# A decoder layer whose kernel plans its own order: loads of inputs get an earliest start, and the stage ranks change

## The chip, the cores and the metric

The kernel runs on one core of a Trainium2 chip. The metric is the device time of one execution in microseconds. Three runs of the kernel before gave 891.12, 892.58 and 895.39 us; the median is 892.58. One more execution was recorded by the hardware profiler, and all views below come from that one.

The core has these engines, each with its own program in order: TensorE (PE; its weight loads are shown apart as PEld), VectorE (DVE), ScalarE (ACT), GpSimd (POOL) and SyncE (SP). SP here only issues transfers. Sixteen DMA engines carry out the transfers that SP and POOL issue.

## The reference

Sixteen sequences of 256 tokens by 256 channels go through one layer, all in float32. There are three sub-layers, each added to its input and then normalised:

```python
x = layernorm(x + attn(x, ...))            # causal depthwise conv, cos/sin features, cumulative sums, gate
x = layernorm(x + xattn(x, ctx, ctx, ...)) # autocorrelation by FFT, top 5 shifts, softmax, rolled values
x = layernorm(x + ffn(x, ...))             # 8 experts: (x V) * cumsum(x W), router softmax, projection by U
```

In `ffn`, two branches are computed, of which the second works on inputs that went through one more matrix, `W_inv`:

```python
Q = x @ W_Q.T; K = x @ W_K.T; invQ = Q @ W_inv.T; invK = K @ W_inv.T
out = fused_branch(Q, K, V_fwd, W_fwd, U_fwd, ...) + alpha_bi * fused_branch(invQ, invK, W_inv_exp, V_inv, U_inv, ...)
return out @ W_O.T
```

The kernel multiplies the weight matrices of this chain together first, which it calls folding, so that each branch needs one product per side and expert.

## The kernel before

**The work.** The sequences are handled in eight pairs. For each pair there are seven stages: `front` (input projection, convolution, score weights), `body` (features, cumulative sums, output projection, first layernorm), `context` (spectra of the context's keys and values), `back`, `attention` (the second sub-layer), `router` and `experts` (the third). `fold_weights` runs once. Contexts depend on no other stage; for pairs 1 to 7 (`AHEAD`, line 50) the spectra are stored to scratch tensors in HBM (`kf_away`, `vf_away`) and `back` loads them again before attention.

**The order.** The code of the stages does not run in the order in which it is written. The objects V, S, G, T and Y (for DVE, ACT, POOL, PE and SP) only take notes: each call becomes an operation (`Op`) with a duration, a latency, its predecessors, and a rank from `PLACES` (line 39), which for every stage holds a length and one begin for each pair. `Work.run` (line 385) then plans and issues. It makes three passes (`PASSES`). In each, `forward` (line 264) is a list scheduler: each engine takes the operation of the lowest rank among those that can run, where an operation needs its predecessors done and places free for its tiles. `backward` (line 375) then finds for each operation the latest time at which it could run, walking the operations from the last end to the first and keeping the order on each engine; these times are the ranks of the next pass. The first pass has the ranks of `PLACES`. The pass with the shortest planned span is issued. Each engine's program is then fixed; on the chip, only semaphores for data and buffers hold it up.

**Tiles.** Many tiles share one tag of 18 places, "slab": the raw weights of folding, context tiles (`ct`, `bothc`, `specc`, `ks`), and expert tiles (`e`, `wb`, `h`, `fwT`). Line 407 limits how many of each kind may hold a place. `x` has 7 buffers (`load_x`, line 456), and `xT` has one (line 550).

**The loads of inputs.** On SP's queue are `xT` (one for each pair, 512 KB), `ct` (one for each sequence, 256 KB, line 845) and `in_proj_w`. On POOL's queue are `x` (one for each sequence, 256 KB), the constants and weights of lines 462 to 468 and 716 to 745, and the raw weights of folding (lines 772 and 776). SP also issues the spreads that copy rows of one tile over many partitions of another: `sn` and `ge` (from `zc` and `g`), `ph`, `vh` and `wb`. POOL also issues the stores and reloads of the spectra and the stores of the output.

In the profile nearly every operation has line 399, since the planner issues them all there; tiles tell them apart. `bothc` is made by POOL from `ct`; `w_ps` are the products of folding, which ACT copies out to `w_v`, `w_c`, `w_h` and `u_o`; `sc_ps` and `in_ps` are front's products with `xT`.

Of the kernel before, what the change touches and what calls it, by code (L numbers as in the profile page):

```python
# [36 lines left out]


PLACES = {
    "front": (0.8, 0.85, 4.2, 3.65, 3.95, 4.75, 6.55, 6.1, 7.7),  # L40
    "body": (0, 0.25, 1.4, 3.7, 2.25, 4.35, 5.1, 6.55, 7.1),
    "ctx": (0.55, 0.83, -0.15, 0.45, 0.55, 0.8, 1.0, 1.25, 1.25),
    "back": (0.35, -1.45, -1.5, -2.45, -2.05, 0.65, 1.35, 2.8, 3.6),
    "att": (0.5, 0.6, 0.75, 1.4, 0.05, 4.0, 4.45, 5.55, 6.85),
    "router": (1.75, 1.4, 0.1, 3.0, 3.15, 4.1, 5.5, 7.8, 6.9),
    "expert": (1.03, 3.85, 4.55, 5.7, 5.95, 7.65, 8.25, 8.8, 10.25),
    "fold": (2.4, 0.61),
}
EARLY, SLABS, XT_BUFS, ZC_BUFS, KBUFS, VBUFS, X_BUFS = 3, 18, 1, 6, 2, 3, 7
AHEAD = range(1, NP)  # L50
# [28 lines left out]
class Op:  # L79


    def __init__(self, k, eng, rank):
        self.k, self.eng, self.rank = k, eng, rank
        self.parts, self.mm, self.pre, self.then, self.tiles = [], [], {}, [], []
        self.table, self.shape, self.lock, self.size, self.dur, self.lat = None, None, False, 0, 0.0, 0.0


class Clock:
# [24 lines left out]
class Work:  # L113
# [3 lines left out]


    SETS = {AF.Exp: 0, AF.Sin: 1, AF.Silu: 1, AF.Gelu: 2, AF.Sqrt: 3}
    LEAD = {"PE": 0, "DVE": 85, "ACT": 103, "POOL": 40, "SP": 0}  # L120
    LATE = {"PE": 33, "DVE": 35, "ACT": 35, "POOL": 80, "SP": 40}

# [61 lines left out]
    def note(self, eng, op, issue, args, kw):  # L184
        aps = [v for v in list(args) + list(kw.values()) if isinstance(v, bass.AP)]
        out = kw.get("out", aps[0])
        ins = [v for v in aps if v is not out]
        o = self.last
        if not (eng == "PE" and o and o.eng == "PE" and (self.joins or o.tiles[-1] == out.tensor.name)):
            o = Op(len(self.ops), eng, self.rank)  # L190
            self.ops.append(o)
        self.last = o
        o.parts.append((issue, args, kw))
        d, lat, o.lock = self.cost(eng, op, out, ins)
        if eng == "PE":
            r, c = ins[0].ap[0][1], self.columns(ins[0])
            r0, c0 = ins[0].offset // math.prod(ins[0].tensor.shape[1:]), out.offset // math.prod(out.tensor.shape[1:])
            cells = [(i, j) for i in range(r0 // 32, (r0 + r + 31) // 32) for j in range(c0 // 32, (c0 + c + 31) // 32)]
            o.mm.append((d, cells))
            o.shape = r, c  # L200
        else:
            o.dur, o.lat = d, lat
        if op == "dma_start":
            o.size = 4 * self.columns(out) * out.ap[0][1]
        if op == "activation":
            o.table = self.SETS.get(args[2])
        for ap in ins + [out]:
            t = ap.tensor
            if not hasattr(t, "tag"):
                continue  # L210
            write = ap is out
            p0, p1, f0, f1 = self.box(ap)
            self.tiles.setdefault(t.name, (t, []))[1].append(o)
            keep = []
            for a in self.users.get(t.name, ()):
                q, w, a0, a1, b0, b1 = a
                meets = q is not o and a0 < p1 and p0 < a1 and b0 < f1 and f0 < b1
                if meets and (w or write):
                    o.pre[q] = o.pre.get(q, False) or w
                if not (write and meets and p0 <= a0 and a1 <= p1 and f0 <= b0 and b1 <= f1):  # L220
                    keep.append(a)
            keep.append((o, write, p0, p1, f0, f1))
            self.users[t.name] = keep

            if t.name in o.tiles:
                o.tiles.remove(t.name)
            o.tiles.append(t.name)
# [33 lines left out]
            return 35 if raw and o.eng != "PE" else -q.lat  # L261
        return self.LATE[o.eng]

    def forward(self, rank):
        need = {o: len(o.pre) for o in self.ops}
        ready = dict.fromkeys(self.ops, 0.0)
        can = {e: sorted((rank[o], o.k, o) for o in self.ops if o.eng == e and not o.pre) for e in self.LEAD}
        free = dict.fromkeys(self.LEAD, 0.0)
        held = {"DVE": 0.0, "POOL": 0.0}
        empty = {tag: [0.0] * n for tag, n in self.slots.items()}  # L270
# [3 lines left out]
        last, taken = {}, {}  # L274
# [3 lines left out]
        def wanted(o):  # L278

            names = [name for name in o.tiles if name not in taken]  # L280
            for name in list(names):
                names += [n for n in self.after[name] if n not in taken and n not in names]
            return names

        def room(o):

            r, names = ready[o], wanted(o)
            for name in names:
                tag, kind = self.tiles[name][0].tag, self.kind[name]
                places = empty[tag]  # L290
                n = 1 if len(names) == 1 else sum(self.tiles[q][0].tag == tag for q in names)
                if len(places) < n:
                    return None
                if kind and (name not in turn[kind][-n:] or share[kind] < 1):
                    return None
                if not kind and not self.takes(name, starts):
                    return None
                r = max(r, (places[0] if len(places) == 1 else sorted(places)[n - 1]) + 40)
            return max([r] + [taken[name] for name in o.tiles if name in taken])

        landed = {"SP": 0.0, "POOL": 0.0}
        starts, order = {}, []
        while len(order) < len(self.ops):
            pick = None
            for e, ops in can.items():
                if pick is not None and free[e] >= pick[0]:
                    continue

                t, best, later = free[e], None, []
                for key, k, o in ops:  # L310
                    if best is not None and key > best[0]:
                        break
                    r = room(o)
                    if r is None:
                        continue
                    key += self.swap if o.table is not None and o.table != table else 0.0
                    if r > t:
                        later.append((r, key, k, o))
                    elif best is None or (key, k) < best[:2]:
                        best = key, k, o  # L320
                if best is None:
                    if not later:
                        continue
                    t = min(later, key=lambda c: c[0])[0]
                    best = min(c[1:] for c in later if c[0] <= t)
                if pick is None or t < pick[0]:
                    pick = t, best[2]
            if pick is None:
                raise RuntimeError("nothing can go on")
            t, o = pick  # L330
            e = o.eng
            can[e].remove((rank[o], o.k, o))
            for name in wanted(o):
                tag, kind = self.tiles[name][0].tag, self.kind[name]
                slot = min(empty[tag])
                empty[tag].remove(slot)
                taken[name] = slot + 40
                if kind:
                    turn[kind].remove(name)
                    share[kind] -= 1  # L340
            if o.table is not None and o.table != table:
                t, table = t + 1283, o.table
            if e == "PE" and o.shape != shape:
                t, shape = t + 93, o.shape
# [11 lines left out]
            for name in o.tiles:  # L356
                left[name] -= 1
                last[name] = max(last.get(name, 0.0), end)
                if not left[name]:
                    empty[self.tiles[name][0].tag].append(last[name])  # L360
                    if self.kind[name]:
                        share[self.kind[name]] += 1
            for q in o.then:
                ready[q] = max(ready[q], end + self.gap(o, q, q.pre[o]))
                need[q] -= 1
                if not need[q]:
                    insort(can[q.eng], (rank[q], q.k, q))
        return order, starts, max(end for t, end in starts.values())

    def takes(self, name, starts):  # L370
# [13 lines left out]

    def run(self, passes):
        self.prepare()
        rank, best = {o: o.rank for o in self.ops}, None
        for n in range(passes):
            order, starts, span = self.forward(rank)
            if best is None or span < best[0]:  # L390
                best = span, order, starts
            rank = self.backward(starts, span)
        self.span = best[0]
        self.give(best[1], best[2])

# [863 lines left out]
```

## Time and profile before

| what | value |
|---|---|
| median of three runs | 892.58 us (891.12 to 895.39) |
| the profiled execution | 892.24 us, of which the span is 890.5 us |
| granted TensorE clock, mean of the span | 0.98 |
| matmuls, other instructions of DVE, ACT, POOL | 4500; 1230, 861, 269 |
| DMA traffic | 99.46 MB, mean 112 GB/s |
| traffic by slice, first four slices of 22 us | 294, 346, 101, 56 GB/s |
| of the engines' time, whole span | SP's queue 35.0%, POOL's queue 10.8% |
| of the engines' time, first 45 us | SP's queue 33.9%, POOL's queue 62.5% |
| shares of the chain that ended last | PE 48%, DVE 19%, ACT 15%, DMA 9%, issue 6%, SP's queue 2% |

The page gives for each engine the time in which it was busy, and then cuts the span into 40 slices: each digit is the busy share of a slice in tenths. The row PEclk is the clock that TensorE was granted, in tenths of full speed. The chain of waits is followed back from the last instruction to whatever released each step; its rows give a start, a duration and the step. A row of the list of waits names the engine that waited and its tile, then whom it waited for, the total in microseconds, how often, and the longest.

### The profile page before, as it was taken

How to read it: one execution, taken by the hardware profiler on the slowest of the kernel's cores; microseconds unless marked ns; L12 is line 12 of the kernel's file. 1: busy time of each engine (PE TensorE's matmuls, PEld its weight loads, DVE VectorE, ACT ScalarE, POOL GpSimd, SP SyncE). 2: the span in 40 equal slices, each digit the busy share in tenths (PEclk: the TensorE clock that was granted, in tenths of full speed). 3: DMA queues.
4: the chain of work that ended last, by engine and by line, in shares of the span. 5: the costliest groups of instructions: out<-in, count | busy, mean ns of one | idle time of the engine just before them, and what ended most of it. 6: DMA issues, size and time to landing. Idle time of an engine off the chain costs nothing.

```text
span 890.5 us, 12540 instructions
## 1 busy us (share of the span) xinstructions
PE 830.9 (93%) x4500; PEld 492.8 (55%) x4500; DVE 712.3 (80%) x1230; ACT 581.8 (65%) x861; POOL 239.3 (27%) x269
## 2 busy tenths in 40 slices
PE   4689998999989999998999989997999999999994
PEld 2345554554537655674557535573566557666554
DVE  6489698878999999799898999997999976364241
ACT  3668966896966785689857887677596942322401
POOL 8640485621320123121212311030323111120000
PEclk9899999999999999999999989999999999999998
DMA  9942758443656246514652637236463160050050
GB/s 294 346 101 56 211 130 237 135 140 81 142 120 134 56 97 141 142 36 107 142 119 72 166 67 145 49 63 127 124 138 79 41 149 18 1 118 1 24 96 24
DMA packets 52382, 99.46 MB, mean 112 GB/s; under 512 B 6592, under 2 KB 18928, under 8 KB 52320
## 3 DMA queue, kind: packets, MB, share of 16 engines
q1 hardware_dynamic: 42640, 67.65, 35.0%
q0 software_dynamic: 9680, 31.01, 10.8%
q8 instruction: 35, 0.57, 0.3%
q14 instruction: 27, 0.22, 0.1%
HBM read 28.38 MB, written 11.53 MB: 45 GB/s over the span
## 4 chain that ended last, share of the span: by engine, by line
PE 48%; DVE 19%; ACT 15%; DMA 9%; issue 6%; SPq 2%; POOL 0%; POOLq 0%; DVEq 0%; ACTq 0%
PE u_ps L399 10%; PE v_ps L399 9%; PE c_ps L399 7%; PE h_ps L399 4%; DVE cs L399 4%; ACT cs L399 4%; DVE sn L399 3%; DMA sn<-zc 3%; ACT L399 3%; DVE zc L399 3%; ACT sn L399 3%; PE wo_ps L399 2%; PE roll_ps L399 2%; DMA xT<-in_xT 2%; SPq L399 2%
## 5 line engine op out<-in xcount | busy, mean ns | idle before, releaser
L399 ACT ACT_TABLE_LOAD x89 | 114.2, 1283 | 46.2 <-DVE flmv L399 33.9
L399 PE MATMUL v_ps<-fxT,w_v 128*128 128x512 f32 x256 | 122.9, 614 | 2.5 <-ACT wf L399 2.5
L399 PE MATMUL c_ps<-fcT,w_c 128*128 128x512 f32 x256 | 119.3, 600 | 0.0
L399 PE MATMUL u_ps<-u_o,e 128*128 128x256 f32 x512 | 116.2, 380 | 0.5 <-ACT h L399 0.5
L399 PEld LDWEIGHTS u_ps<-u_o,e 128*128 128x128 f32 x512 | 96.3, 190 | 15.8 <-issue 1.5
L399 DVE SCALAR_TENSOR_TENSOR zc<-in_ps,pv,zc 128x255 f32<-128x255 f32 (+4 forms) x144 | 76.5, 558 | 3.3 <-ACT zc L399 2.7
L399 PEld LDWEIGHTS v_ps<-fxT,w_v 128*128 128x128 f32 x256 | 48.2, 195 | 55.7 <-issue 49.6
L399 PEld LDWEIGHTS c_ps<-fcT,w_c 128*128 128x128 f32 x256 | 47.8, 192 | 54.1 <-issue 50.2
L399 DVE TENSOR_TENSOR_SCAN cs<-again,cs 128x1024 f32<-128x1024 bf16 x32 | 77.3, 2415 | 0.1
L399 DVE TENSOR_TENSOR_SCAN sn<-again,sn 128x1024 f32<-128x1024 bf16 x32 | 76.7, 2396 | 0.1
L399 POOL TENSOR_TENSOR x<-x,bo 128x512 f32<-128x512 f32 x16 | 30.3, 1896 | 140.7 <-DVE bothx L399 125.1
L399 PE MATMUL in_ps<-xT,in_proj_w 128*32 128x256 f32 (+1 forms) x576 | 62.0, 407 | 3.0 <-DVE zc L399 2.0
L399 PE MATMUL kv_ps<-Wkv,specc 128*128 128x512 f32 x128 | 59.2, 601 | 3.9 <-ACT specc L399 3.8
L399 POOL TENSOR_TENSOR pp<-qf,kf 128x256 f32<-128x256 f32 (+1 forms) x32 | 45.0, 1425 | 57.5 <-ACT qf L399 55.4
L399 PE MATMUL h_ps<-fxT,w_h 128*128 128x512 f32 x128 | 59.7, 603 | 0.7 <-ACT specx L399 0.7
L399 ACT ACTIVATE sn<-sn,theta_col 128x512 f32<-128x512 f32 x64 | 44.4, 714 | 21.1 <-DMA sn<-zc 21.1
L399 DVE TENSOR_TENSOR e<-e,v_ps 128x512 f32<-128x512 f32 x64 | 42.7, 673 | 17.0 <-PE v_ps L399 16.9
L399 DVE TENSOR_TENSOR sn<-sn,ge 128x1024 f32<-128x1024 f32 x32 | 41.3, 1292 | 10.3 <-ACT sn L399 7.4
L399 DVE SCALAR_TENSOR_TENSOR cs<-cs,sn 128x1024 f32<-128x1024 f32 x32 | 40.7, 1272 | 10.1 <-ACT cs L399 10.0
L399 POOL TENSOR_TENSOR t<-vf,wf 128x256 f32<-128x256 f32 x32 | 24.6, 788 | 89.5 <-ACT wf L399 64.6
L399 ACT ACTIVATE ge<-sn 128x1024 f32<-128x1024 f32 x32 | 33.8, 1055 | 22.4 <-DVE cs L399 13.8
L399 POOL TENSOR_TENSOR g<-g,zc 128x512 f32<-128x512 f32 x16 | 22.1, 1380 | 96.8 <-ACT g L399 92.9
(217 smaller groups left out, 1633.4 us busy)
## 6 DMA issues: line engine op xcount, KB each, us to landing
sn<-zc SPq DMA_DIRECT2D x64, 256.0 KB
ge<-g SPq DMA_DIRECT2D x64, 256.0 KB
wb<-fwT SPq DMA_DIRECT2D x64, 256.0 KB
ct<-in_ctx SPq DMA_DIRECT2D x16, 256.0 KB
xT<-in_xT SPq DMA_DIRECT2D x8, 512.0 KB
x<-in_x POOLq DMA_DIRECT2D x16, 256.0 KB, 5.0
ph<-sc SPq DMA_DIRECT2D x64, 64.0 KB
vh<-sv SPq DMA_DIRECT2D x32, 128.0 KB
```

What stands on the lines that cost most here:

```text
L399: call(*args, **kw)
```

## The change

Three things change. First, the planner marks as a fetch every transfer whose source is no tile, that is, an input in HBM. In the second and third pass a fetch can't begin before its latest time from the pass before, less 40 us. Second, all eight rows of `PLACES` have new numbers (the length of "fold" is used nowhere, its begin is). Third, `forward` keeps what it found for an engine or an operation until something that was looked at has changed.

```diff
 PLACES = {
-    "front": (0.8, 0.85, 4.2, 3.65, 3.95, 4.75, 6.55, 6.1, 7.7),
-    "body": (0, 0.25, 1.4, 3.7, 2.25, 4.35, 5.1, 6.55, 7.1),
-    "ctx": (0.55, 0.83, -0.15, 0.45, 0.55, 0.8, 1.0, 1.25, 1.25),
-    "back": (0.35, -1.45, -1.5, -2.45, -2.05, 0.65, 1.35, 2.8, 3.6),
-    "att": (0.5, 0.6, 0.75, 1.4, 0.05, 4.0, 4.45, 5.55, 6.85),
-    "router": (1.75, 1.4, 0.1, 3.0, 3.15, 4.1, 5.5, 7.8, 6.9),
-    "expert": (1.03, 3.85, 4.55, 5.7, 5.95, 7.65, 8.25, 8.8, 10.25),
-    "fold": (2.4, 0.61),
+    "front": (0.8, 0.8, 4.55, 3.6, 3.95, 4.75, 6.6, 6.1, 7.7),
+    "body": (0.05, -0.05, 1.4, 3.7, 2.25, 4.4, 5.45, 7.05, 7.25),
+    "ctx": (0.75, 1.48, 0.15, 1.2, 1.3, 1.55, 1.8, 1.9, 2.05),
+    "back": (1.75, -2.35, -2.3, -4.2, -4.15, -1.0, -0.45, 1.1, 2.25),
+    "att": (0.25, 0.6, 0.85, 1.35, 0.3, 3.95, 4.45, 5.7, 7.0),
+    "router": (1.6, 1.35, -0.85, 3.0, 2.5, 3.65, 5.5, 7.7, 6.95),
+    "expert": (1.03, 3.85, 4.5, 5.6, 5.95, 7.45, 8.1, 8.95, 10.25),
+    "fold": (1.0, 0.66),
 }
...
+    AHEAD = 40000.0
...
         if op == "dma_start":
             o.size = 4 * self.columns(out) * out.ap[0][1]
+            o.fetch = not any(hasattr(i.tensor, "tag") for i in ins)
...
-    def forward(self, rank):
+    def forward(self, rank, late=None):
         need = {o: len(o.pre) for o in self.ops}
-        ready = dict.fromkeys(self.ops, 0.0)
+
+        ready = {o: max(0.0, late[o] - self.AHEAD) if late and o.fetch else 0.0 for o in self.ops}
...
+        found, looked, seen, stuck, settled = {}, {}, set(), {}, {}
+        version = dict.fromkeys(empty, 0)
...
-        rank, best = {o: o.rank for o in self.ops}, None
+        rank, late, best = {o: o.rank for o in self.ops}, None, None
         for n in range(passes):
-            order, starts, span = self.forward(rank)
+            order, starts, span = self.forward(rank, late)
             if best is None or span < best[0]:
                 best = span, order, starts
-            rank = self.backward(starts, span)
+            rank = late = self.backward(starts, span)
```

In the lines left out of `forward`, `found` holds an engine's next choice, `stuck` an operation's lack of a place together with the `version` of that tag, and `settled` the earliest start of an operation that needs no new place. They are dropped when a place of the tag is taken or freed, or when a predecessor ends.

More of the change, by code (lines that the diff above doesn't have):

```diff
@@ L85, in __init__ @@
         self.table, self.shape, self.lock, self.size, self.dur, self.lat = None, None, False, 0, 0.0, 0.0
+        self.fetch = False
 class Clock:
@@ L289, in room @@
                 tag, kind = self.tiles[name][0].tag, self.kind[name]
+                seen.add(tag)
                 places = empty[tag]
+                stuck[o] = tag, version[tag]
                 n = 1 if len(names) == 1 else sum(self.tiles[q][0].tag == tag for q in names)
@@ L296, in room @@
                 if not kind and not self.takes(name, starts):
+                    seen.add(None)
+                    stuck[o] = None
                     return None
                 r = max(r, (places[0] if len(places) == 1 else sorted(places)[n - 1]) + 40)
-            return max([r] + [taken[name] for name in o.tiles if name in taken])
+            r = max([r] + [taken[name] for name in o.tiles if name in taken])
+            stuck[o] = None
+            if not names:
+                settled[o] = r
+            return r
         landed = {"SP": 0.0, "POOL": 0.0}
+        found, looked, seen, stuck, settled = {}, {}, set(), {}, {}
+        version = dict.fromkeys(empty, 0)
         starts, order = {}, []
@@ L307, in forward @@
                     continue
+                if e in found:
+                    if pick is None or found[e][0] < pick[0]:
+                        pick = found[e][:2]
+                    continue
+                seen = looked[e] = set()
                 t, best, later = free[e], None, []
@@ L312, in forward @@
                         break
-                    r = room(o)
+                    r = settled.get(o)
                     if r is None:
-                        continue
+                        b = stuck.get(o)
+                        if b and version[b[0]] == b[1]:
+                            seen.add(b[0])
+                            continue
+                        r = room(o)
+                        if r is None:
+                            continue
                     key += self.swap if o.table is not None and o.table != table else 0.0
@@ L325, in forward @@
                     best = min(c[1:] for c in later if c[0] <= t)
+                found[e] = t, best[2]
                 if pick is None or t < pick[0]:
@@ L332, in forward @@
             can[e].remove((rank[o], o.k, o))
+            changed = {None}
+            found.pop(e)
             for name in wanted(o):
@@ L337, in forward @@
                 taken[name] = slot + 40
+                changed.add(tag)
                 if kind:
@@ L360, in forward @@
                     empty[self.tiles[name][0].tag].append(last[name])
+                    changed.add(self.tiles[name][0].tag)
                     if self.kind[name]:
@@ L367, in forward @@
                     insort(can[q.eng], (rank[q], q.k, q))
+                    found.pop(q.eng, None)
+            for tag in changed:
+                if tag is not None:
+                    version[tag] += 1
+            for f in list(found):
+                if looked[f] & changed:
+                    del found[f]
         return order, starts, max(end for t, end in starts.values())
```

## Prediction

> **What bounds the kernel now.** I read the page's busy rows and slices first, then the chain of waits in time order, a table of 4 us windows, TensorE's waits, the timeline of GpSimd's DMA issues, and the groups by tile.
>
> ```profile
> span 890.5 us, 12540 instructions
> PE 830.9 (93%) x4500; PEld 492.8 (55%) x4500; DVE 712.3 (80%) x1230; ACT 581.8 (65%) x861; POOL 239.3 (27%) x269
> PE   4689998999989999998999989997999999999994
> PEclk9899999999999999999999989999999999999998
> DMA  9942758443656246514652637236463160050050
> ```
>
> TensorE is the bound nearly everywhere. Its idle time is 890.5 - 830.9 = 59.6 us. By windows of about 22 us, 8.4 us of it lie before the first matmul, 13.1 between 8.4 and 70 us, 11.3 in the last window (the last layernorm and store), and the remaining 26.8 are scattered. Only in the first two slices (22 us each) are the DMA engines full, and there the clock and TensorE's row are low too. So holding loads back can pay at the start; elsewhere there is little traffic to relieve.
>
> ```profile
> 22.57 12.69 DMA ph<-sc
> 35.33 12.51 DMA xT<-in_xT
> ...
> 107.43 2.76 DMA ph<-sc
> ...
> 609.26 6.72 DMA xT<-in_xT
> ```
>
> Columns: start, duration. The same transfers on the chain cost 2.76 and 6.72 us in quieter stages: crowding adds 9.9 us to the first and 5.8 to the second.
>
> ```profile
> 26.00:30.00 4.00, 1.44 (x12) 0.68 (x4) 1.85 (x5) 2.79 (x4) 1.97 (x3) 1.00 1.02 373
> 30.00:34.00 4.00, 1.13 (x4) 0.68 (x4) 0.75 (x1) 3.27 (x5) 3.26 (x6) 0.77 1.05 335
> 34.00:38.00 4.00, 3.32 (x4) 1.17 (x4) 0.86 (x3) 3.97 (x7) 2.20 (x3) 0.50 1.05 308
> ...
> 46.00:50.00 4.00, 2.12 (x22) 1.53 (x23) 4.00 (x3) 2.06 (x4) 1.19 (x1) 0.91 0.31 109
> 50.00:54.00 4.00, 4.00 (x10) 2.02 (x9) 4.00 (x3) 1.11 (x3) 3.27 (x2) 0.67 0.00 0
> ```
>
> After the window and its length: busy us of PE, PEld, DVE, ACT, POOL; granted clock; DMA share; GB/s. Between 22 and 50 us TensorE idles 10.1 us, and at the reduced clock it loses busy time x (1 - clock) = 3.9 us between 30 and 54.
>
> ```profile
> PE w_ps L399 <- ACT w_v L399: 6.1, 2, 3.2
> PE sc_ps L399 <- DMA xT<-in_xT: 3.4, 1, 3.4
> ```
>
> Of the idle time, 3.4 us is the wait for pair 1's xT. The 6.1 us are fold products waiting for ScalarE to empty a bank; the timeline shows ScalarE itself held until 27.18 us by sn's transfer (4.81 us idle). Both waits end in a transfer.
>
> **Which loads move, and how far.** Tagged as fetches are 80 DMAs: 16 ct, 16 x, 8 xT and 40 for weights. Nothing on chip waits on a clock: a held load merely stands later in its queue's program, the queues being POOL's and SP's. The instruction count of each kind stays. A load may begin at late - 40 us in passes 2 and 3, not in pass 1.
>
> The backward pass keeps each engine's order. So a fold matmul's latest time is about its own time plus what TensorE still idles or loses to the clock before the tail. After 21.7 us that is 59.6 - 11.4 - 11.3 = 37 us, up to 48 with the clock's 11 (busy time x (1 - clock) over the windows). After 64 us it is 27 to 35.
>
> ```profile
> 5.05 1.43 POOL L399 DMA_DIRECT2D x<-in_x  x2
> ...
> 14.22 0.71 POOL L399 DMA_DIRECT2D raw<-in_W_Q  x1
> ...
> 32.25 1.43 POOL L399 DMA_DIRECT2D x<-in_x  x2
> ...
> 38.73 1.09 POOL L399 DMA_DIRECT2D raw<-in_U_fwd  x2
> ...
> L399 DVE TENSOR_TENSOR x<-x,out_ps x16: 656/679/690, 107.7 to 741.3; 128x512 f32<-128x512 f32 x16
> ```
>
> - U_fwd and U_inv (issued 38.7 to 41.5) are first read at 64.2. Latest: 64 + 27..35 - 7 (landing) = 84..92; less 40: 44..52. They move 5 to 13 us later. The five x loads before them (32.3 to 37.8) can be no later than they are in POOL's order, and move some 11. Together with bt this takes 2.1 + 1.3 + 0.1 = 3.5 MB out of the stage from 32 to 45 us, in which about 330 GB/s x 13 us = 4.3 MB flowed. Their 10 issues of 0.54 to 0.78 us, some 6.4 in all, go past bothc on POOL's queue into 44 to 52, where POOL is busy 1.19 and 3.27 us in the two 4 us windows shown; I cost them at nothing, since POOL has 0.2 us of work from 58 to 89. If that cover fails, a bothc starts 6 us later, and its context's TensorE work with it.
> - W_Q, the first fold weight: 21.7 + 37..48 - 5 - 40 = 14..25, against 14.2 now: 0 to 11 us later. The first x pair and the attention weights (5.05 to 14.2; 2.65 MB, first read at 102.9 to 172.4 but for Wo) stand before it, so they are held no longer than it is. In this group the loads that could wait 60 us are bounded by neighbours that cannot.
>
> **The sum**, against this execution (892.24 us; 1.7 outside the span; median 892.58):
>
> 1. xT of pair 1 lands in 6.7 instead of 12.5: TensorE's 3.4 us go. Bounds 0 and 5.8. Late next there: the front's bias and convolution on ScalarE and VectorE.
> 2. ph and ge overlap the thinned stage only at their end. Of 9.9 us on the chain I take 1.5 (x traffic of 32.25 to 34.9, 0.79 MB, is 2.3 us at 346 GB/s and is shared with what stays); bounds 0 and 9.9. The 6.1 us of bank waits lie before 32 us, so I leave them.
> 3. Clock: without the hole at 47 us, the 46 to 54 windows keep full speed: 2.12 x 0.09 + 4.00 x 0.33 = 1.5 us. Bounds 0 and 3.9.
> 4. PLACES: "ctx" starts 0.3 to 0.8 later and is longer, "back" 0.8 to 2.1 earlier and is longer, "fold" 0.05 later; the other stages shift by up to 0.95. These ranks only seed pass 1. The trace shows no such order. Bounds: the 26.8 us of scattered idle time given back, or as much again lost. Nearest row: 140 to 158 us, where contexts, sn and ge meet and TensorE idles 4.1 us; an sn transfer took 10.21 us there against 5.06 at 541.59. I take a quarter, 1 us.
> 5. The caches in forward (found, settled, stuck, version) run on the host and issue nothing: 0. Should one alter a choice, it is order again, inside term 4's bounds.
>
> Sum: 3.4 + 1.5 + 1.5 + 1 = 7.4; 892.2 - 7.4 = 884.8: **885 us**.
>
> The Trainium skill, "DMA: Bandwidth & Descriptors", section Queues, rings and completion order, says that each DMA engine takes turns packet by packet between the queues that have work. By that estimate, an empty POOL queue can at most double SP's rate: xT to 6.3 and ph to 6.3, 6 us each, where the rows say 5.8 and 9.9. This trace has POOL's queue at 62.5% and SP's at 33.9% of the engines' time in the first 45 us, not equal turns.
>
> Against the change speaks "TensorE: Matmul & The Clock Gate", section HAM oscillation — how this bites in real kernels: a TensorE gap over about 3.4 us halves its clock. Here gaps of 2.93 and 3.18 us already go with clocks of 0.77 and 0.50. By the rule a held fold weight that opens such a gap costs 1.7 us more for each window of 3.4 us at half clock, an estimate from that page.
>
> **Rivals.**
> - *Held fold weights starve TensorE* (slower). Decides once W_Q is issued after 21.7 - 4.8 (its landing) = 16.9 us; the slack above allows up to 25. Held 11 us, the 5.8 us of fold work that TensorE now does between 21.7 and 33 have no input; they move into stages that are full, with 2 to 3 us of clock as lost from 30 to 42: +8.5, less 1 from thinner traffic: 900. For: after 70 us TensorE has no room to take the work. Against: where slack is under 40, nothing is held. Beside it, POOL's queue has waits of up to 32.8 us (x waiting for bothx): an x load behind one spends most of its 40 us margin.
> - *It doesn't do what it says*: the best of the three plans is the first, unheld, one, or the slack is under 40 throughout. Then only ranks differ: 892, from 888 to 897. For: the slack is so near to 40. Against: the five x loads, 75 us early.
> - *The order gains more than the loads*: new ranks for all eight stages regain half of the 26.8 scattered us: 13.4 + 7.4 = 21, giving 871. For: DVE and ACT are 41% and 28% busy from 757 to 868 us, so work could shift. Against: of TensorE's waits after 67 us only one ends in a held kind of load (xT, 4.7 us at 616), and it was issued late, not early.
>
> **How the numbers follow.** Forecast 0.40 (879 to 888); order gains 0.22 (862 to 879); no change 0.18 (888 to 897); starved 0.20 (897 to 910). Faster by over 0.5%, which is about what a measurement of this kernel can tell from no change, means under 888: 0.40 + 0.22 = 0.62; within 0.18; slower 0.20. Leaving out about a tenth at either end: 866 to 902. The forecast's own range is 879 to 888.
>
> **What would show it.** In the changed profile: x and U loads on POOL's timeline after 43 us; DMA's second slice under 9; pair 1's xT near 6.7 us; no sc_ps wait near 48; clock above 0.9 from 46 to 54; W_Q still issued before 17. A first w_ps matmul after 25 us means the starved rival. Slices 0 to 2 alike, and a change only after 70 us, mean that the order did it. The forecast is wrong if TensorE's idle time before 70 us (21.5 with the start) does not fall by 4 to 7 us, or if idle time after 70 moves by more.

## The result and the profile after

Twenty executions of the changed kernel have a median of 896.07 us (892.87 to 901.32), twenty of the kernel before 892.05 us (886.55 to 898.4). The ratio is 1.0049, with a 95% interval from 1.0029 to 1.007: **slower by half a per cent, some 4 us**, where 885 was forecast. All ratios here and below leave out four executions in a slower state: three of the kernel before, near 899 us, and one of expert_row_new, 1067.64 us at a granted clock of 0.768. The profiled execution took 894.54 us. The page of the changed kernel (the planner's issue line, 399 before, is 438 here, and 404 to 445 in the experiments):

```profile
span 892.8 us, 12553 instructions
...
PE 832.0 (93%) x4500; PEld 491.1 (55%) x4500; DVE 711.4 (80%) x1230; ACT 595.8 (67%) x871; POOL 252.4 (28%) x269
...
PE   5598999998999999999899899999999999999994
...
PEclk9699999999999999999999999999999999999998
DMA  9953667454644264615552572546261361050050
```

ScalarE is 14 us busier, with 99 activation table loads of 1283 ns where there were 89. The other profiles with the new ranks have 95 to 100, the rest 88 or 89, so that comes with the order. The two full DMA slices are still full, and the low clock slice is still there. TensorE idles 892.8 - 832.0 = 60.8 us, against 59.6 before, and 20.6 of them lie before 70 us, against 21.5. The start, where the forecast wanted 4 to 7 us less, gave back 0.8. That is within the spread of single executions: ranks_no_hold below, whose program is the same up to 183 us, idles 19.2 us before 70. The timeline of GpSimd's DMA issues in the changed kernel says why the start is as full as it was:

```profile
5.07 1.43 POOL L438 DMA_DIRECT2D x<-in_x  x2
...
12.10 0.71 POOL L438 DMA_DIRECT2D raw<-in_W_Q  x1
...
32.25 0.73 POOL L438 DMA_DIRECT2D x<-in_x  x1 [0.21 <-issue]
...
37.85 1.11 POOL L438 DMA_DIRECT2D raw<-in_U_fwd  x2
47.76 0.54 POOL L438 DMA_DIRECT2D raw<-in_U_inv  x1 [8.80 <-PE w_ps L438]
```

Of the loads that the forecast wanted later, hardly one is. The first x pair is issued at 5.07 (5.05 before). All seven early x loads are out by 36.7 us, W_Q is 2 us earlier than before, U_fwd 0.9 earlier. Only U_inv comes later, and its bracket shows that it waited 8.80 us for a buffer that fold products were still reading. Wkv, f_dft and the two loads of biases from b_qkvo do stand 5 to 6 us later (Wkv at 31.30 instead of 26.21); that is the new order, since the planner starts them well after their earliest times.

What did change at the start is the order, since the ranks are new. The list of TensorE instructions from 20 to 45 us, changed kernel (start, duration, in brackets the idle time before and what ended it):

```profile
21.55 5.43 PE L438 MATMUL w_ps<-raw 128*128 128x512 f32 x16
32.63 1.94 PE L438 MATMUL bv_ps<-Wo,bv 128*32 128x256 f32 x16 [5.66 <-ACT w_v L438]
38.74 1.93 PE L438 MATMUL sc_ps<-xT,w_sc 128*32 128x256 f32 x16 [4.17 <-DVE b_dc L438]
40.60 3.42 PE L438 MATMUL in_ps<-xT,in_proj_w 128*128 128x512 f32 x4
```

xT of pair 1 is now issued at 27.61 instead of 35.33, so TensorE's 3.4 us of waiting for it have gone, as forecast. In their place stand two longer gaps, 5.66 and 4.17 us, earlier. The table of 4 us windows of the changed kernel (columns as in the prediction) shows what they do to the clock:

```profile
26.00:30.00 4.00, 0.98 (x5) 0.52 (x3) 0.00 (x0) 3.06 (x5) 3.28 (x6) 0.99 0.99 314
30.00:34.00 4.00, 1.37 (x16) 0.59 (x16) 2.17 (x5) 3.90 (x6) 2.76 (x5) 0.50 1.06 300
...
38.00:42.00 4.00, 3.26 (x18) 1.52 (x19) 0.96 (x3) 3.63 (x5) 0.96 (x2) 0.50 1.05 366
...
46.00:50.00 4.00, 4.00 (x17) 2.96 (x16) 4.00 (x3) 3.16 (x7) 1.05 (x2) 1.00 0.23 60
50.00:54.00 4.00, 3.68 (x37) 1.19 (x35) 4.00 (x4) 2.70 (x4) 0.02 (x1) 1.00 0.34 86
```

From 46 to 54 the clock is full, as forecast, but from 30 to 42 it is halved. Busy time x (1 - clock), summed over 4 us windows from 18 to 66 us, is 3.4 us, against 3.9 before. The start moved its holes; it did not lose them.

A hole that the kernel before does not have comes right after it. TensorE's busy time by stage, first two rows after, then the same two stretches of before (busy us of PE, PEld, DVE, ACT, POOL; clock; DMA share; GB/s):

```profile
67.00:111.00 44.00, 39.18 (x263) 22.56 (x262) 37.57 (x55) 40.44 (x63) 14.05 (x15) 1.00 0.47 124
111.00:250.00 139.00, 128.93 (x732) 72.19 (x734) 119.64 (x176) 110.83 (x176) 64.28 (x70) 0.99 0.58 145
```

```profile
67.00:111.00 44.00, 43.27 (x276) 25.39 (x275) 35.15 (x49) 40.78 (x63) 9.97 (x14) 1.00 0.50 134
111.00:250.00 139.00, 129.99 (x783) 71.27 (x781) 124.84 (x181) 108.67 (x176) 64.95 (x69) 1.00 0.56 144
```

Between 67 and 111 us the changed kernel idles 4.8 us, the one before 0.7. By 250 us its TensorE has 4.3 us less busy time (0.8 more at 67, less 4.1, less 1.1) and 1258 matmuls behind it instead of 1324; from 250 to 690 its busy time gains 3.1 again in these two executions. So the hole is plain, but that it is what the time pays for is a reading, not shown.

### The profile page after: what moved, and what is told of

Its sections match the earlier page's. It is cut to its first block, busy times and chain, and to the rows that moved or that the text cites. A ratio compares the mean times of both kernels' runs of the same rounds, so it can differ in the third digit from the quotient of the medians.

```text
span 892.8 us, 12553 instructions
## 1 busy us (share of the span) xinstructions
PE 832.0 (93%) x4500; PEld 491.1 (55%) x4500; DVE 711.4 (80%) x1230; ACT 595.8 (67%) x871; POOL 252.4 (28%) x269
## 4 chain that ended last, share of the span: by engine, by line
PE 37%; DVE 18%; ACT 12%; issue 5%; DMA 3%; POOL 1%; SPq 0%; POOLq 0%; DVEq 0%; ACTq 0%
PE v_ps L438 8%; PE c_ps L438 7%; PE u_ps L438 6%; DVE cs L438 5%; DVE sn L438 4%; ACT L438 3%; PE h_ps L438 3%; PE roll_ps L438 2%; DMA sn<-zc 2%; PE wo_ps L438 2%; ACT cs L438 2%; ACT sn L438 2%; DVE zc L438 2%; DVE e L438 1%; PE ss L438 1%
## 5 line engine op out<-in xcount | busy, mean ns | idle before, releaser
L438 ACT ACT_TABLE_LOAD x99 | 127.0, 1283 | 48.2 <-DVE flmv L438 33.9
L438 PE MATMUL v_ps<-fxT,w_v 128*128 128x512 f32 x256 | 120.3, 599 | 0.1
L438 DVE SCALAR_TENSOR_TENSOR zc<-in_ps,pv,zc 128x255 f32<-128x255 f32 (+3 forms) x144 | 75.8, 561 | 4.1 <-ACT zc L438 3.8
L438 POOL TENSOR_TENSOR x<-x,bo 128x512 f32<-128x512 f32 x16 | 34.9, 2184 | 137.1 <-DVE bothx L438 92.2
L438 PE MATMUL in_ps<-xT,in_proj_w 128*32 128x256 f32 (+1 forms) x576 | 64.8, 413 | 5.2 <-DVE zc L438 5.2
L438 PE MATMUL h_ps<-fxT,w_h 128*128 128x512 f32 x128 | 61.7, 619 | 2.2 <-ACT fxT L438 2.1
L438 POOL TENSOR_TENSOR g<-g,zc 128x512 f32<-128x512 f32 x16 | 25.7, 1605 | 107.3 <-ACT g L438 107.3
L438 POOL TENSOR_TENSOR t<-vf,wf 128x256 f32<-128x256 f32 x32 | 29.3, 935 | 79.5 <-ACT wf L438 54.1
```

What stands on the lines that cost most here:

```text
L438: call(*args, **kw)
```

## The experiments

**Theory**, formed from the profile after: the earliest times bind nothing where DMA is full, and the new ranks alone cost the 4 us. **Rival 1**: the hold itself costs it, by pushing loads past their readers later on. **Rival 2**: nothing was there to gain, since the crowding of the start is harmless. All ratios are to the kernel before, measured on the same chip beside it, with 95% intervals. "Planned us" are times in the planner's own plan.

A figure from the kernel itself is used along with the profile: the spans of its three plans. Before, these are 862.65, 854.32 and 853.96 us, and the third is issued; after, 865.39, 853.33 and 860.43, and the second is.

**1. ranks_no_hold.** The new ranks, without the hold (this `AHEAD` belongs to the class `Work`; the list of pairs on line 50 has the same name):

```diff
-    AHEAD = 40000.0
+    AHEAD = 1.0e9
```

> The new ranks with the margin set so wide that no load is held. Every engine's program is the same as in the changed kernel up to about 200 us; after that they part. If the new ranks made the difference: about 896 us, ratio to the kernel before 1.003 to 1.007, and the same stages before 200 us as in the changed kernel. If the hold made it: about 892 us, ratio 1.000 within 0.002.

Measured: 896.68 us, ratio 1.0043 (1.0018 to 1.0069). The loss is there without the hold. On all five engines the program is that of the changed kernel up to 183 us, where an xT is issued that the changed kernel issues at 216.88. TensorE's row between 67 and 111 us agrees to 0.01 us with the one after:

```profile
67.00:111.00 44.00, 39.19 (x261) 22.19 (x260) 36.80 (x55) 40.42 (x65) 12.09 (x13) 1.00 0.48 125
```

So the ranks cost it, and the hold does nothing that can be measured beside them.

**2. hold_old_ranks.** The changed kernel with the eight rows of `PLACES` as they were before.

> The kernel before with the hold alone: old ranks, margin 40 us. The planner's own span for it is 862.6 us, against 854.0 for the kernel before and 853.3 for the changed one; the held passes lose to the first. If chip time follows the planned span: 892 + 8.6 = about 901 us, ratio 1.01. If the plan's last 1% is lost in what the plan doesn't model: anywhere from 890 to 905. If the hold by itself relieves the first 45 us: under 890; I do not expect that, since the first pass, which has no hold, is the one that is issued.

Measured: 897.1 us, ratio 1.0048 (1.0028 to 1.0069). The hold alone is not free either: its three plans are 862.65, 862.62 and 862.66 us, so the improvement of the later passes is lost. The expectation was wrong on one point: the second plan, with the hold, is the shortest and is issued, not the first. Beside the second plan of the kernel before, the first transfer that stands elsewhere is one load of xT, held from 84.9 to 90.8 planned us. The planner gave up 8.7 us; the chip lost about half of it. The two parts do not add up (1.0043 and 1.0048 apart, 1.0049 together): each merely leads to another plan.

**3. hold_30.** The changed kernel with a shorter lead, so that the hold binds:

```diff
-    AHEAD = 40000.0
+    AHEAD = 30000.0
```

> The changed kernel with a margin of 30 us in place of 40: 25 loads start when their hold ends, where 9 do so at 40; the planner's own span is the same, 853.3 us. If a hold that binds costs time on the chip: 898 to 905. If it helps: 888 to 893. If only the ranks count: 896, ratio to the kernel before 1.002 to 1.007.

Measured: 895.06 us, ratio 1.003 (1.0005 to 1.0054). Now 25 of the 80 loads start at their earliest time in the issued plan (9 at 40 us), U_fwd and U_inv among them, but these only 1.5 to 7 planned us later than at 40. Against ranks_no_hold it is 1.6 us less, inside the intervals: no gain shown.

**4. loads_moved.** The kernel before, its plan and all else kept; seven early x loads (256 KB each), Wq, c_mean, c_corr, f_roll, c_roll and out_proj_w, 3.7 MB together (not 3.9, as the expectation has it), are issued later on POOL's queue, 25 planned us before their first reader:

```diff
     def give(self, order, starts):
-        for o in order:
+        at = {}
+        for n, o in enumerate(order):
+            at[o] = starts[o][0], n
+            if o.size and o.parts[0][2]["in_"].tensor.name in (...) and starts[o][0] < 45000.0:
+                at[o] = max(starts[o][0], min(starts[q][0] for q in o.then) - 25000.0), n
+        for o in sorted(order, key=at.get):
```

> The kernel before with one edit: the first seven x loads and Wq, c_mean, c_corr, f_roll, c_roll and out_proj_w (3.9 MB) are issued 25 planned us before their first reader, later in GpSimd's queue; the order of everything else stays on every engine. If crowding of the transfers in the first 45 us costs what the prediction's first three terms say: ph and xT on the chain fall from 12.7 and 12.5 us to under 8, TensorE's idle time before 70 us falls from 21.5 by 4 to 8 us, and the time falls to 884 to 889, ratio 0.990 to 0.996. If the crowding is covered anyway: ratio 0.998 to 1.002, with the idle time found again later. If the moved loads come late behind GpSimd's waits: over 895, with out_ps or q_ps waiting for a load.

Measured: 888.56 us, ratio 0.9943 (0.9914 to 0.9973): **faster**. This is the diff's idea, done to the loads that the diff's own rule leaves alone. Page and TensorE's waits from 8 to 67 us of this kernel:

```profile
span 886.6 us, 12550 instructions
...
PE 826.1 (93%) x4500; PEld 491.6 (55%) x4500; DVE 710.5 (80%) x1230; ACT 581.3 (66%) x861; POOL 231.1 (26%) x269
...
DMA  7862768453766265415561638044654160050050
```

```profile
PE sc_ps L404 <- DMA w_sc<-in_w_sc: 9.3, 1, 9.3
PE w_ps L404 <- DVE bo L404: 4.1, 1, 4.1
PE w_ps L404 <- ACT w_v L404: 2.4, 1, 2.4
```

The first DMA slice falls from 9 to 7, W_Q is issued at 7.68 instead of 14.22, pair 1's xT at 31.15 instead of 35.33. The 3.4 us wait for xT is gone, the bank waits fall from 6.1 to 2.4 us, and a wait that ends with VectorE, which has waited 3.8 us for ph, comes up in their place (4.1 us). The time is where the expectation had it, the idle time is not: before 70 us TensorE idles 18.6 us, 2.8 less than before and not 4 to 8. Busy time x (1 - clock) from 18 to 66 us falls from 3.9 to 2.7.

Rival 2 falls: a thinner start does save time. That W_Q goes out 6.5 us earlier is not what does it: the first fold product starts at 22.36 us here and at 21.68 before, and in neither list does a fold product wait for its weights. The transfers themselves get quicker: from the last issue of the second set of ph to VectorE's read of it, 12.6 us pass before (25.3 to 37.9), 9.9 here (26.5 to 36.4), and 6.2 in more_moved below (26.9 to 33.1).

**5 and 6. only_x_moved, only_weights_moved.** The same edit with the list cut to `in_x`, and to the six others.

> The kernel before with only the seven x loads moved (1.8 MB, five of them issued at 32 to 37 us). The prediction put most of the gain on loads of that late group, through xT of pair 1. If so: at least two thirds of what loads_moved gained, ratio 0.996 or less. If the gain comes from the early group (5 to 13 us), which lies ahead of the first sn and ph: ratio 0.998 to 1.000.

> The kernel before with only Wq, c_mean, c_corr, f_roll, c_roll and out_proj_w moved (2.1 MB, issued at 6.5 to 12 us). If the early group counts: ratio 0.994 to 0.997, the fold weights issued some 5 us earlier, ScalarE's wait for sn under 2 us. If the late group counts: 0.998 to 1.000.

Measured: 888.83 us, ratio 0.9952 (0.9925 to 0.998), and 888.88 us, ratio 0.9973 (0.9946 to 1.0001). The x loads alone (1.8 MB) gain; for the weights alone (also 1.8 MB, not 2.1) a gain is likely but not certain. The two medians are the same and the intervals overlap, so which group matters more is not shown. The product of the two ratios, 0.9925, lies inside the interval of loads_moved, so nothing speaks against their adding up.

**7. more_moved.** As loads_moved, and also U_fwd, U_inv, bt, wot and w2t, issued 8 planned us before their first reader, and Wkv and V_inv, 12 us before.

> loads_moved, and besides U_fwd, U_inv, bt, wot and w2t issued 8 planned us before their first reader, and Wkv and V_inv 12. TensorE still idled 4.1 us at 37.5 us there, behind VectorE's wait of 3.8 us for ph. If that wait is crowding by the fold weights: it falls under 1 us, TensorE's idle time before 70 us falls by 2 to 4 more, ratio 0.990 to 0.993. If these weights then come too late: w_ps waits for a raw load at 50 to 70 us, ratio 0.995 or more.

Measured: 887.45 us, ratio 0.9937 (0.9906 to 0.9967), not to be told from loads_moved. Its page:

```profile
span 886.1 us, 12552 instructions
...
PE 831.9 (94%) x4500; PEld 493.6 (56%) x4500; DVE 710.6 (80%) x1230; ACT 581.9 (66%) x861; POOL 230.8 (26%) x269
```

The rows of the first 67 us, more_moved, loads_moved and before (columns as above):

```profile
0.00:67.00 67.00, 52.45 (x303) 29.11 (x304) 48.20 (x91) 47.17 (x75) 29.97 (x51) 1.00 0.79 224
0.00:67.00 67.00, 48.36 (x283) 26.41 (x284) 43.67 (x88) 41.37 (x64) 33.79 (x52) 0.95 0.77 220
0.00:67.00 67.00, 45.55 (x269) 23.75 (x270) 43.01 (x85) 38.04 (x60) 44.44 (x62) 0.92 0.80 247
```

TensorE idles 54.2 us, 5.4 less than before, and 14.6 before 67 us, 6.9 less, at full clock throughout. VectorE's wait for ph fell from 3.8 us in loads_moved to 0.4, as expected if it was crowding, and TensorE's 4.1 us behind it went. So the start gains more, but the time of the whole kernel does not show it. In loads_moved, the profiled execution has no less idle time in all (60.5 us) but a higher clock (0.988 against 0.980).

**8. new_ranks_moved.** The changed kernel with the edit of loads_moved.

> The changed kernel with the same loads moved as in loads_moved. If the crowding of the first 45 us and the cost of the new ranks are separate terms, the two add: 0.9943 x 1.0049 = 0.9992, about 892 us. If the new ranks are slower because of the crowding, the move takes their cost away too: 0.994 or less, about 887. If the move helps only in the old order: 1.003 or more.

Measured: 892.28 us, ratio 0.9997 (0.9972 to 1.0022). The product of the two effects, 0.9943 x 1.0049 = 0.9992, lies well inside, and the two other outcomes lie outside: the loss by the order and the gain from a thinner start add up. The hole from 67 to 111 us is still there (5.4 us idle).

**9. contexts_earlier.** Why does the new order idle at 67 to 111 us? In the changed kernel's POOL timeline the contexts, which the new ranks begin later, wait for their loads:

```profile
81.19 2.70 POOL L438 TENSOR_TENSOR bothc<-ct 128x256 f32<-128x256 f32 x2 [10.19 <-DMA ct<-in_ctx]
90.69 1.43 POOL L438 TENSOR_TENSOR bothc<-ct 128x256 f32<-128x256 f32 x2 [6.79 <-DMA ct<-in_ctx]
```

The edit issues the ct loads that the plan starts between 60 and 100 us 12 planned us earlier:

```diff
...
+            if o.size and o.parts[0][2]["in_"].tensor.name == "in_ctx" and 60000.0 < starts[o][0] < 100000.0:
+                at[o] = starts[o][0] - 12000.0, at[o][1]
...
```

> The changed kernel, plan and ranks as they are; only the issue order on SP differs: the context loads that the plan starts between 60 and 100 us are issued 12 planned us earlier, ahead of the sn and ph spreads that they stand behind. In the profile of the changed kernel POOL waits 10.2 and 6.8 us for ct at 81 and 91 us, and TensorE idles 4.8 us between 67 and 111 us, against 0.7 before. Theory A, the late contexts hold TensorE through their loads: the two waits fall under 3 us together, TensorE idles under 2 us in that stretch, and the time falls by 3 to 4 us from 896, to a ratio of about 1.001 to the kernel before. Rival B, the new order as a whole is what costs the time and the loads are only where it shows: the waits for ct go, the idle time comes back at other steps, and the ratio stays within 1.003 to 1.006.

Measured: 896.88 us, ratio 1.0042 (1.0022 to 1.0062). Both waits for ct are gone, and nothing is won: TensorE idles 5.8 us from 67 to 111. **My theory A fell here.** TensorE's waits in that stretch, contexts_earlier:

```profile
PE kv_ps L442 <- ACT specc L442: 2.6, 2, 2.1
PE y L442 <- DVE cs L442: 1.6, 1, 1.6
PE in_ps L442 <- DVE zc L442: 1.6, 1, 1.6
```

and in the changed kernel:

```profile
PE kv_ps L438 <- ACT specc L438: 2.3, 2, 1.8
PE in_ps L438 <- DVE zc L438: 1.6, 1, 1.6
PE y L438 <- DVE cs L438: 0.8, 1, 0.8
```

The same three waits in both, and in the kernel before only kv_ps for specc, 0.7 us: they are steps of short chains from engine to engine with no other TensorE work beside them. That no other work was at hand is argued, not shown. The first dft_ps of a context runs at 79.1 us in the changed kernel, against 48.9 before. All six profiled kernels with the new ranks idle 4.5 to 5.8 us between 67 and 111, body_row_old below (4.8) among them; the others, expert_row_new (1.0) among them, idle 0.7 to 2.0. So the new row "body" is not needed for the hole and the new row "expert" alone does not make it; the other rows were not separated, since a change of one row changes the whole plan. Nor is such a hole the only way to lose: hold_old_ranks idles 2.0 us there and is as slow.

**10 and 11. body_row_old, expert_row_new.** Do small differences between planned spans mean anything? The changed kernel without the hold and with the old row "body", planned at 851.8 us, the shortest of all; and the kernel before with the new row "expert", planned at 855.5, longer than before.

> The changed kernel without the hold and with one row of ranks, body, as it was before. The planner's span is 851.8 us, the shortest of all: 853.0 with all new ranks, 854.0 with all old ones. Theory A, differences of one or two planned us say nothing of the chip: the time is anywhere in 889 to 898, most likely near the 896.7 of the new ranks, since all other rows are the new ones. Rival B, the chip keeps the order of the plans: the time is below 892, the kernel before's, at a ratio of 0.996 to 0.999.

> The kernel before with one row of ranks, expert, replaced by the new one, and no hold. The planner's span is 855.5 us, 1.6 longer than with the old row. Theory A, such differences say nothing of the chip: anywhere in 888 to 898. Rival B, the chip keeps the order of the plans: 893 to 894, ratio about 1.002.

Measured: 896.09 us, ratio 1.0025 (0.9999 to 1.005), and 892.96 us, ratio 0.9974 (0.9947 to 1.0001). The shortest plan is likelier slower than faster, the longer one likelier faster. All orders with the issue left as planned:

| order | planned span, us | measured ratio |
|---|---|---|
| body_row_old | 851.8 | 1.0025 |
| ranks_no_hold | 853.0 | 1.0043 |
| after | 853.3 | 1.0049 |
| hold_30 | 853.3 | 1.003 |
| before | 854.0 | 1 |
| expert_row_new | 855.5 | 0.9974 |
| hold_old_ranks | 862.6 | 1.0048 |

Within 4 us, the planned span does not order the measured times. A longer plan by 8.7 us was measurably slower.

**12. expert_row_moved.** The row of experiment 11 and the loads of more_moved together.

> The kernel before with two changes that each gave a ratio under 1: the new row of ranks for expert (0.9974) and the early loads issued later in their queues, 25, 12 or 8 planned us before their first reader, as in more_moved (0.9937). Theory A, crowding of the first 45 us is a cost of its own beside the order of the work, so the two add up: ratio 0.991, bounds 0.988 to 0.995. Rival B, the new order gained because its start happens to be less crowded, so that moving the loads as well brings no more than it does alone: 0.993 to 0.998.

Measured: 883.94 us against 894.15 of the kernel before on the same chip, ratio 0.989 (0.9844 to 0.9935): faster than both kernels, and the product of its parts (0.9974 x 0.9937 = 0.9911) lies inside the interval. Theory A held; of rival B's range (0.993 to 0.998) only the edge is inside. Its page:

```profile
span 882.3 us, 12550 instructions
...
PE 827.1 (94%) x4500; PEld 490.8 (56%) x4500; DVE 709.6 (80%) x1230; ACT 582.1 (66%) x861; POOL 226.3 (26%) x269
...
PEclk9999999999999999999999989999999999999998
DMA  7882767643755365415561638145643450050050
```

The low clock slice of the start (8 before and 6 after, in the second digit) is a 9 here, the two later 8s are as before, and the first DMA slice is at 7.

## Why the prediction was wrong

**The step that failed is "Which loads move, and how far".** The prediction took the margin of a fold load from the chip's execution: TensorE's idle and clock losses still to come, 27 to 48 us, and so the x and U loads were to move 5 to 13 us. But the planner sees only its own plan. What it had there in the issued pass (planned us, from its own figures):

```
load      earliest   planned start   latest (pass before)   first reader
W_inv_exp      0.3            15.5                   40.3           37.5
x (pair 1)     3.4            21.1                   43.4          175.4
U_fwd         21.4            29.9                   61.4           45.5
U_inv         32.2            35.1                   72.2           56.2
```

Each of these loads starts 22 to 37 us ahead of its latest time. That is under 40, so its earliest time lies before its start and holds nothing back. In the whole plan 9 of the 80 loads start at their earliest time: a ct at 98 us and eight others later.

Two terms of the prediction's margin were too large. For U_fwd it had 25.5 us from issue to first reader (38.7 to 64.2), where the plan has 15.6 (29.9 to 45.5). And it took TensorE's idle time still to come for the margin of that reader, 27 to 35 us. The plan has such idle time too: TensorE idles 64 of the 865 us of the pass before the issued one, and 38 of them lie between that reader and 820 us. Yet the reader's margin there is 22.2 us. So the idle time of one engine overstates the margin of an operation on it; through which engine the rest is bound was not traced. With 6.3 us for the landing and the issue behind it taken off, 15.6 + 22.2 - 6.3 = 31.5 us, which is under 40; the prediction's 25.5 + 27 - 7 = 45.5 was over it, and so the whole group seemed to move. The prediction named this as the rival *It doesn't do what it says*, "the slack is so near to 40", at 0.18, and gave it 888 to 897. That was the case, and 896.07 lies there. The prediction's remark that "the loads that could wait 60 us are bounded by neighbours that cannot" was right, and is why the rule leaves so much untouched: the backward pass keeps POOL's order, so the latest time of an x load, whose reader is 85 us away or more, is set by the fold weight behind it.

**Term 1, xT, 3.4 us.** The wait went, but by the ranks, and 5.66 and 4.17 us of other gaps took its room. In loads_moved it went too: xT was issued 4.2 us earlier and its reader came at 45.7 without a wait, so that it landed in 6.7 us is not shown.

**Term 2, ph and ge, 1.5 us.** Nothing in the changed kernel's start was thinned. In loads_moved VectorE's waits for ph fell from 5.8 to 3.8 us, near the 1.5; but ScalarE's waits for sn fell too, from 5.5 to 1.0, and the bank waits fell from 6.1 to 2.4. I had left these out because they lie before 32 us, which was misread: the second of them ran from 31.5 to 34.7. A start that is thinned from its first microseconds relieves them.

**Term 3, the clock, 1.5 us.** The 46 to 54 windows did get full speed; the same loss reappeared from 30 to 42.

The sum of these three, 3.4 + 1.5 + 1.5 = 6.4 us, is near what the runs that really thin the start gain, 5.1 (loads_moved, 893.67 - 888.56) and 6.2 us (more_moved, 893.64 - 887.45). Part of that is luck, since they move other loads, from 5 us on, and relieve waits that the sum left out. The mechanism, that a crowded start costs time, was right; the diff does not set it off.

**Term 4, the ranks, +1 us.** Measured: 3 to 4 us lost (ranks_no_hold, 896.68 against 893.67). The bounds of 26.8 us to either side held it, but the sign was a guess with one row behind it, and the only stage that stands out afterwards lies elsewhere, at 67 to 111 us. As the hold moved no early load, this term was the whole result.

**Term 5, the caches, 0.** Supported: with the old ranks and no hold the new `forward` gives the same three planned spans as before, with every transfer planned at the same time. It was not run by itself.

**The other rivals.** *Starved folds*: W_Q went out at 12.10 and the first fold product ran at 21.55, so no. *Order gains more*: the order lost. The prediction's last test, idle time before 70 us falling by 4 to 7 or else the forecast is wrong, gave the answer: 0.8.

**The rule that spoke against the change.** The clock halves here after TensorE stood still from 26.98 on: 0.99 from 26 to 30, 0.50 from 30. The same sixteen sc_ps products took 607 to 634 ns each at 38.7 us, against 379 ns before. The Trainium skill, "TensorE: Matmul & The Clock Gate", section HAM oscillation — how this bites in real kernels, puts the limit at idle gaps of about 3.4 us; the 5.66 us gap agrees. Yet the clock was down within 3 us of its begin, and before, gaps of 2.93 and 3.18 us already went with clocks of 0.77 and 0.50, so here the limit isn't that sharp.

**Open.** Why the new order is worse is read as far as the three waits between 67 and 111 us, not traced to a rank. The ten more table loads, 12.8 us of ScalarE's time, are a rival that no run separates. Whether the changed kernel's later, binding earliest times (after 98 us) help or harm a little can't be told from 1.0049 and 1.0043.

## What to carry to other kernels

Before crediting a rule that delays work, find out whether it binds: compare its limit with the margin that the planner itself has, in its own times and with its queue order, not with an engine's idle time. When a diff also reshuffles an order that a heuristic made, price that as a few tenths of a per cent of either sign, whatever the planned span says. And crowding at a start is worth removing where loads with readers far away are under way together with urgent transfers, here on the other queue: 3.7 MB moved out of the first 45 us took 0.6% off, with no other edit.

## What was not expected of the hardware

The spread between executions of one kernel goes with the granted clock. Over 103 executions of the kernel before, the span falls by 6.1 us for each 0.01 of mean clock (correlation -0.78). The kernels differ in it too: on one chip, 33 executions of before had a mean of 0.9781, 11 of loads_moved 0.9852. At 6.1 us for 0.01 that is 4.3 us of the 5.2 us between their mean spans (891.5 and 886.3). For more_moved on another chip it is 1.4 of 6.5 us (0.9795 and 0.9818; 891.1 and 884.6). These go together; which brings about which, and why the split differs, was not shown. The changed kernel's loss is not of this kind: its 20 executions had a mean clock of 0.980, and ranks_no_hold had 0.9792 beside 0.9781 of the kernel before.

Thinning POOL's queue did not simply speed up SP's. From 15 to 45 us SP's queue took 32.9% of the engines' time before and 38.0% in loads_moved, while POOL's fell from 68.1% to 40.8%: about a fifth of the time was left free, and ph was still waited for.

The prediction read 62.5% against 33.9% in the first 45 us as unequal turns of the two queues. Counted in packets they were equal; POOL's were larger, 3.1 KB against 1.6. These are the rows of before, POOL's queue first, with packets, MB and share:

```profile
q0 software_dynamic: 3085, 9.42, 62.5%
q1 hardware_dynamic: 3093, 4.95, 33.9%
```
